# Masked self-attention with residual, one core: where the output products, the block turns, the mean and the fetches stand in the hand-written order

## The chip, the core and the metric

The kernel runs on 1 core of one Trainium2 chip. The metric is the device time of one execution in microseconds (us). Before the change it was measured at 685.06 us, the median of 3 runs (682.3 to 690.17). Five engines work side by side, each through a queue of its own in program order: PE (TensorE, matmuls; its weight loads are listed as PEld), DVE (VectorE), ACT (ScalarE), POOL (GpSimd) and SP (SyncE, which here only issues DMAs).

## What is computed

For each of 8 batches, `x` is 512 features by 1024 tokens, and a mask holds 0 or 1 for each token. With 8 heads of 64 features:

```python
xt = jnp.transpose(x, (0, 2, 1))
q = xt @ Wq.T
qh = q.reshape(B, T, NH, dk).transpose(0, 2, 1, 3)
scores = scale * jnp.einsum('bhqd,bhkd->bhqk', qh, qh)
logits = (scores * cmask + (1.0 - cmask) * NEG) * rmask
attn = jax.nn.softmax(logits, axis=-1)
ctx = jnp.einsum('bhqk,bhkd->bhqd', attn, qh)
out = ctx.transpose(0, 2, 1, 3).reshape(B, T, D) @ Wo.T
return x + jnp.transpose(out, (0, 2, 1))
```

`cmask` and `rmask` are the mask along keys and along queries. A masked key gets no weight; a masked query attends evenly to all tokens, so that its result is the mean over the tokens. Queries, keys and values are the same projection.

## The kernel before, in words

**Data.** Only the kept tokens of a batch are computed: up to 543 of them, gathered into NK = 544 columns, whose last column (number 543) holds the mean of all tokens. Every masked token of the batch takes its result from that column. `END` is 32, so a batch has five token blocks: four of 128 and one of 32 (`LAST`, number 4). Everything is float32.

**Turns.** The 8 heads of a batch make 4 pairs, so the work is 32 turns (b, pr), written out by hand under a manual schedule. A turn has five slots, k = 0 to 4. Slot k begins with the scores of one key block (slot 0 of the small block, slots 1 to 4 of blocks 0 to 3): matmuls of L669 and L691 into two PSUM tiles of tag "s" (two buffers, one for each head of the pair), then on ACT one exponential per head (L677), which frees the tile. After the scores, the slot's tasks are issued (`slots_of`, L1010 on), then the loads, searches, gathers and so on that tables in `late` name for (pr, k). Each engine takes its instructions in the order in which they were issued. So the order of calls is the order of the work, and whatever stands ahead of an exponential on ACT delays it.

**What a turn does beside its scores.** Slot 1 makes the values of the next pair. Slot 2 ends the weighted sums of the pair before (`end_attend`) and issues `lengths_of` for the next pair: ACT squares the values (L628), DVE adds them up and takes the maximum (L630, L637), for the bias of the exponentials. Slot 3 projects the first or second half of the queries of the pair after next (`project`, L583); with the second half of it, or with the first half in the turns pr = 2, goes the product of the maxima (`project_with_top`, `turn_top`, L640): PE turns DVE's maxima into the same PSUM bank, ACT copies the queries out (L593, L595), and DVE makes the bias (L649 to L652). After slot 4, `begin_attend` starts the weighted sums (L733) of the turn's own pair. The next turn starts with the scores of the small block (L691), which take the tile that the first head's exponential of slot 4 frees.

**Feature sums.** In slot 3 of the turns pr = 1 (for batch b + 1) and pr = 3 (for b + 2), behind the slot's tasks, ACT adds up four pieces of x (`add_features`, L492). DVE makes the mean's input from them after slot 4 of pr = 1 (`mean_of`, L497 and L499).

**The turns pr = 2.** Here the next batch's token blocks become columns: `collect` turns one block by four PE transposes (L551), and DVE or ACT copies it out (L555). Blocks 0 and 1 are in slot 2, blocks 2, 3 and 4 in slot 3 ahead of the projection with the maxima. Slot 1 has `put_mean`: four products of 128x32 by 128x4 (L566), one for each quarter of the partitions, and one DVE write (L569).

**Output.** `output` (L859) makes one token block of the previous batch: products of all four pairs' contexts with woT (L868), an ACT copy (L878), and DMAs to `od` in DRAM, issued by POOL (L880). Slot 3 of pr = 1 has blocks 0, 1 and LAST, pr = 2 has block 2, pr = 3 block 3, each behind the projection. All but block 0 are called with `wait=True`: their ACT copy is put off until after the scores of the next turn's slot 0. Two PSUM banks of tag "t" and two of tag "a" serve all of this.

**Way back.** Two batches later, POOL fetches the rows of `od` into eight blocks (`fetch`, L982, behind a one-element copy of an exponential, `keep_step`, L978, which ties it to the slot), and DVE turns each and adds x (`finish_blocks`, L942 and L945). The tables FETCH and FINISH give the slots.

**PSUM.** Eight banks: four for the scores, two "t", two "a".

Of the kernel before, what the change touches and what calls it, by code (L numbers as in the profile page):

```python
# [10 lines left out]
F32 = mybir.dt.float32  # L11
I32 = mybir.dt.int32
AF = mybir.ActivationFunctionType
ALU = mybir.AluOpType
AX = mybir.AxisListType
# [6 lines left out]
Q = 32  # L22
# [284 lines left out]
def attention_of_kept_tokens(ctx, tc, x, mask, wq, wo, out, ident, wqT, woT, verdict, flag):  # L307
# [37 lines left out]
    within = keep.tile([P, Q], F32, name="within")  # L345
# [214 lines left out]
    def put_mean(b, pm=None):  # L560

        xcs[b] = sb.tile([P, ND, NK], F32, tag="xc", name=f"xc_{b}", bufs=1)
        if pm is None:
            pm = bank(f"mean_{b}")
        for d in range(ND):
            nc.tensor.matmul(  # L566
                pm[d * Q : (d + 1) * Q, :A], within, xmeans[b][:, d, :], start=True, stop=True
            )
        nc.vector.tensor_scalar(xcs[b][:, :, NK - 1], pm[:, :A], 1.0 / T, None, ALU.mult)  # L569
# [287 lines left out]
    copies, rests = [], deque()  # L857

    def output(b, i, wait=False):  # L859
        n = sizes[i]  # L860
        if i == 0:
            ods[b] = dr.tile([NK, D], F32, tag="od", name=f"od_{b}")
        po = bank(f"po_{b}_{i}")
        parts = P // n
        w = D // parts
        for pr in range(ND):
            for k in range(parts):
                nc.tensor.matmul(  # L868
                    po[k * n : (k + 1) * n, :w],
                    cTs[b, pr][:, i * P : i * P + n],  # L870
                    woT[:, pr, k * w : (k + 1) * w],
                    start=(pr == 0),
                    stop=(pr == ND - 1),
                )

        def copy():
            oc = sb.tile([P, D], F32, tag="oc", name=f"oc_{b}_{i}", bufs=NC)
            nc.scalar.copy(oc[:, :w], po[:, :w])  # L878
            for k in range(parts):
                nc.gpsimd.dma_start(  # L880
                    ods[b][places[i], k * w : (k + 1) * w], oc[k * n : (k + 1) * n, :w]
                )

        if wait:
            copies.append(copy)
        else:
            copy()
# [122 lines left out]
    def slots_of(p):  # L1010
# [7 lines left out]
        def do(k, f, *args):  # L1018
            todo[k].append(lambda: f(*args))
# [19 lines left out]
        if before:  # L1039
            do(0, go_on_attend, before)  # L1040
        if p == 0:
# [18 lines left out]
        elif new:  # L1060
            do(1, mean_with_values)
            do(2, end_attend, before)
            do(2, collect, b + 1, 0, by_vector)
            do(2, collect, b + 1, 1)
            do(2, lengths_of, behind)
            do(3, collect, b + 1, 2, None, "a")
            do(3, collect, b + 1, 3, by_vector, "a")
            do(3, collect, b + 1, 4, by_vector)
            do(3, project_with_top, 0)
# [16 lines left out]
        if pr == 1 and b + 1 == B:  # L1086
            for i in range(LAST - 1):
                do((3, 3, 4)[i], output, b - 1, i)
        elif pr > 0 and 0 < b < B - 1:
            if pr == 1:  # L1090
                do(3, output, b - 1, 0)
            for i in {1: (1, LAST), 2: (2,), 3: (3,)}[pr]:
                do(3, output, b - 1, i, True)
# [30 lines left out]
    def early(n):  # L1124
# [37 lines left out]
        for ri in ris:  # L1162
# [8 lines left out]
            within, ident.rearrange("p (a f) -> p f a", a=A), axis=AX.X, op=ALU.add  # L1171
# [77 lines left out]
    def late(n):  # L1249
# [16 lines left out]
        for hf in range(2):  # L1266
# [15 lines left out]
            (0, 1): (0,),  # L1282
            (0, 2): (1,),
            (0, 3): (2,),
            (0, 4): (3,),
            (1, 0): (4, 5),
            (1, 1): (6, 7),
        }
        FINISH = {(0, 4): (0, 1), (1, 0): (2,), (1, 1): (3, 4), (1, 3): (5, 6), (1, 4): (7,)}
# [4 lines left out]
        for p, pair in enumerate(pairs):  # L1294
# [3 lines left out]
            for k, c in enumerate(order):  # L1298
                scores(pair, c)
                if k == 0:  # L1300
                    for copy in copies:
                        copy()
                    copies.clear()
# [196 lines left out]
```

## Time and profile before

| | |
|---|---|
| profiled execution, device time | 683.56 us |
| its span, first to last instruction | 681.8 us |
| median of the runs | 685.06 us (682.3 to 690.17) |
| mean granted TensorE clock | 0.973 |
| PE matmul busy | 627.0 us (92%) |
| DVE, ACT, POOL busy | 370.6, 386.7, 186.7 us |
| DMA | 116.55 MB, mean 171 GB/s |

How to read it: busy time is given for each engine, and a share of the span beside it. In lists of instructions, `x8` counts them, `[2.38 <-DVE top L637]` says that the engine sat idle for 2.38 us before this one and what released it. In lists of waits, the columns are the total in us, the number of times, and the longest. In rows for stretches of time, `PEclk` is the clock that TensorE was granted, as a share of full speed. Matmuls appear in two passes each, so a product of four matmuls is listed as x8.

### The profile page before, as it was taken

The page shows a single profiled execution, that of the slowest core. Times are in us where ns is not written, and L with a number is a line of the kernel's source. Part 1 is how long each engine was busy: PE and PEld are TensorE (multiplying, and loading weights), DVE is VectorE, ACT ScalarE, POOL GpSimd, SP SyncE. Part 2 cuts the span into 40 slices and gives each one's busy share as a digit, 9 for nine tenths or more (in the row PEclk, how much of TensorE's full clock was granted, in tenths as well). Part 3 has the DMA queues.
Part 4 walks back from the last instruction along what each step waited for, and adds up shares of the span by engine and source line. Part 5 has one row for each costly group of instructions (what it writes and reads, how often), then busy time and mean ns, then how long its engine had stood idle before and what let it go on. Part 6 is the DMA issues. An engine that isn't in the chain of part 4 may idle for free. (4 is left out here: it accounts for less than half of the span.)

```text
span 681.8 us, 15988 instructions
## 1 busy us (share of the span) xinstructions
PE 627.0 (92%) x6140; PEld 382.6 (56%) x6140; DVE 370.6 (54%) x1072; ACT 386.7 (57%) x1026; POOL 186.7 (27%) x313
## 2 busy tenths in 40 slices
PE   5798999999989999899998999799998999999974
PEld 4765665566654566556664566455664666645332
DVE  5446766246575455745576455745656423833742
ACT  3377767665764477574774477464774655536400
POOL 5620310310181103710172102810064102411421
PEclk9999999999997999999998999999998999999995
DMA  7553534443764687647875678648864653357656
GB/s 243 188 196 112 180 114 113 133 133 99 198 208 133 196 194 214 211 127 210 216 208 148 195 169 224 187 124 230 222 179 133 163 139 88 114 164 171 196 163 202
DMA packets 98671, 116.55 MB, mean 171 GB/s; under 512 B 10471, under 2 KB 76519, under 8 KB 98590
## 3 DMA queue, kind: packets, MB, share of 16 engines
q1 hardware_dynamic: 81742, 75.13, 41.5%
q0 software_dynamic: 12624, 38.25, 17.7%
q10 hardware_dynamic: 4224, 2.10, 1.0%
q8 instruction: 49, 0.80, 0.5%
q14 instruction: 32, 0.26, 0.1%
HBM read 72.78 MB, written 42.67 MB: 169 GB/s over the span
## 5 line engine op out<-in xcount | busy, mean ns | idle before, releaser
L677 ACT ACTIVATE e<-s,bias 128x544 f32<-128x544 f32 x256 | 180.5, 710 | 93.8 <-PE s L669 91.2
L669 PE MATMUL s<-qT 64*64 64x272 f32 x2048 | 151.9, 397 | 2.2 <-ACT e L677 0.8
L583 PE MATMUL pq<-xc,wqT 128*128 128x272 f32 x512 | 132.6, 403 | 4.4 <-ACT xc L555 4.4
L733 PE MATMUL av<-e,v 64*64 64x272 f32 x1920 | 130.9, 389 | 0.0
L583 PEld LDWEIGHTS pq<-xc,wqT 128*128 128x128 f32 x512 | 92.3, 190 | 40.0 <-issue 13.6
L880 POOL DMA_DIRECT2D od<-oc x56 | 29.9, 542 | 308.6 <-ACT oc L878 298.5
L868 PE MATMUL po<-woT,cT 128*128 128x512 f32 (+1 forms) x448 | 114.4, 453 | 0.0
L669 PEld LDWEIGHTS s<-qT 64*64 64x64 f32 x2048 | 74.9, 132 | 56.5 <-issue 16.0
L733 PEld LDWEIGHTS av<-e,v 64*64 64x64 f32 x1920 | 75.6, 133 | 37.8 <-issue 1.3
L868 PEld LDWEIGHTS po<-woT,cT 128*128 128x128 f32 (+1 forms) x448 | 50.2, 157 | 55.0 <-issue 48.3
L593 ACT COPY qT<-pq 128x272 f32<-128x272 f32 x64 | 24.7, 386 | 86.5 <-PE pq L640 45.1
L630 DVE TENSOR_REDUCE len<-sq 128x10 f32<-128x640 f32 x32 | 26.2, 818 | 81.1 <-ACT sq L628 81.1
L982 POOL DMA_INDIRECT g<-od,block_origin x56 | 57.3, 1024 | 29.8 <-DMA od<-oc 13.6
L677 ACT ACTIVATION_READ_ACCUMULATOR e<-s,bias 128x1 f32 x256 | 50.1, 196 | 0.0
L942 DVE STREAM_TRANSPOSE o<-g 128x512 f32<-128x512 f32 x56 | 39.3, 702 | 16.3 <-DMA g<-od,block_origin 16.0
L538 POOL DMA_INDIRECT xin<-xd,source x40 | 39.4, 984 | 14.3 <-DMA woT<-in_L_cond_Wq_dram 5.5
L945 DVE TENSOR_TENSOR xr<-o,xr 128x512 f32<-128x512 f32 x56 | 39.0, 696 | 1.9
L878 ACT COPY oc<-po 128x512 f32<-128x512 f32 (+1 forms) x35 | 17.5, 519 | 35.1 <-PE po L868 35.1
L473 DVE STREAM_TRANSPOSE xt<-x 128x1024 f32<-128x1024 f32 x28 | 34.8, 1242 | 4.0 <-DMA xd<-xt 3.6
L978 POOL COPY step<-e 1x1 f32<-1x1 f32 x75 | 16.5, 220 | 73.1 <-ACT e L677 72.6
L492 ACT ACTIVATE junka<-x 128x512 f32<-128x512 f32 x56 | 35.4, 631 | 1.3
L649 DVE TENSOR_REDUCE m<-pq 128x1 f32<-128x128 f32 x28 | 8.2, 292 | 50.3 <-ACT qT L595 33.7
(174 smaller groups left out, 702.8 us busy)
## 6 DMA issues: line engine op xcount, KB each, us to landing
xd<-xt SPq DMA_DIRECT2D x120, 128.0 KB
x<-in_x_dram SPq DMA_DIRECT2D x56, 256.0 KB
xr<-in_x_dram SPq DMA_DIRECT2D x28, 512.0 KB
out_dram<-xr SPq DMA_DIRECT2D x24, 512.0 KB
rb<-row SPq DMA_DIRECT2D x60, 160.0 KB
od<-oc POOLq DMA_DIRECT2D x28, 256.0 KB, 3.2
rank<-ranks SPq DMA_DIRECT2D x6, 512.0 KB
x<-in_x_dram POOLq DMA_DIRECT2D x8, 256.0 KB, 4.0
```

What stands on the lines that cost most here:

```text
L473: nc.vector.transpose(xt.rearrange("p k (d f) -> p k d f", d=ND), xs[b][r][:, :, at : at + n].rearrange("p d (k t) -> p k d t", t=Q),)
L492: nc.scalar.activation(junk, xs[b][r][:, d, :], AF.Copy, accum_out=xbars[b][:, d, r : r + 1])
L538: nc.gpsimd.indirect_dma_start(out=xin[:n, :], out_offset=None, in_=xds[b], in_offset=bass.IndirectOffsetOnAxis(ap=searches[b][2][:n, i : ...
L583: nc.tensor.matmul(pq[:, :KH], wqT[:, d, pr * P : (pr + 1) * P], xcs[b][:, d, cols], start=(d == 0), stop=(d == ND - 1),)
L669: nc.tensor.matmul(ss[h][r * DK : (r + 1) * DK, hf, :KH], qT[heads[h], c * P + r * DK : c * P + (r + 1) * DK], qT[heads[h], queries[hf]], ...
L677: nc.scalar.activation(e[:, :, h, :], ss[h][:, :, :KH], AF.Exp, bias=bias, scale=SCALE, accum_out=sums[pair[1] % 2][:, h, c : c + 1],)
L733: nc.tensor.matmul(avs[pair][hf][head, :KH], v[keys, c, head], e[keys, hf, h, :], start=(c == 0 and not crossed), stop=(c == LAST - 1 and ...
L868: nc.tensor.matmul(po[k * n : (k + 1) * n, :w], cTs[b, pr][:, i * P : i * P + n], woT[:, pr, k * w : (k + 1) * w], start=(pr == 0), stop=( ...
L880: nc.gpsimd.dma_start(ods[b][places[i], k * w : (k + 1) * w], oc[k * n : (k + 1) * n, :w])
L942: nc.vector.transpose(o.rearrange("p k t -> p (k t)"), gs[b, i])
L945: nc.vector.tensor_tensor(to, o, to, ALU.add)
L982: nc.gpsimd.indirect_dma_start(out=g, out_offset=None, in_=ods[b], in_offset=bass.IndirectOffsetOnAxis(ap=block_origin[:, b, i : i + 1], a ...
```

## The change

1. `output` no longer puts off its ACT copy. The list `copies`, and the loop that emptied it behind slot 0's scores, are gone.
2. In the turns pr = 1 and pr = 3 the output blocks stand at the head of slot 3's tasks, ahead of the projection with the maxima; in pr = 2 they stand behind the five collects and ahead of that projection. The last batch's pr = 1 has blocks 0 and 1 at the head of slot 3 too; its block 2 stays in slot 4.
3. In pr = 2, all five collects are in slot 3, blocks 0, 1, 2 and 4 copied by DVE, block 3 by ACT, and `lengths_of` comes behind them.
4. The mean: `within` is a 128x128 matrix (four copies of the 128x32 one), and one product of 128x128 by 128x16 takes the place of four; four DVE writes of 32 partitions each take the place of one.
5. FETCH and FINISH name other slots.

```diff
         if pm is None:
             pm = bank(f"mean_{b}")
+        nc.tensor.matmul(
+            pm[:, : ND * A],
+            within,
+            xmeans[b].rearrange("p d a -> p (d a)"),
+            start=True,
+            stop=True,
+        )
         for d in range(ND):
-            nc.tensor.matmul(
-                pm[d * Q : (d + 1) * Q, :A], within, xmeans[b][:, d, :], start=True, stop=True
-            )
-        nc.vector.tensor_scalar(xcs[b][:, :, NK - 1], pm[:, :A], 1.0 / T, None, ALU.mult)
+            rows = slice(d * Q, (d + 1) * Q)
+            nc.vector.tensor_scalar(
+                xcs[b][rows, :, NK - 1], pm[rows, d * A : (d + 1) * A], 1.0 / T, None, ALU.mult
+            )
...
-        def copy():
-            oc = sb.tile([P, D], F32, tag="oc", name=f"oc_{b}_{i}", bufs=NC)
-            nc.scalar.copy(oc[:, :w], po[:, :w])
...
-        if wait:
-            copies.append(copy)
-        else:
-            copy()
+        oc = sb.tile([P, D], F32, tag="oc", name=f"oc_{b}_{i}", bufs=NC)
+        nc.scalar.copy(oc[:, :w], po[:, :w])
+        for k in range(parts):
+            nc.gpsimd.dma_start(ods[b][places[i], k * w : (k + 1) * w], oc[k * n : (k + 1) * n, :w])
...
         if before:
             do(0, go_on_attend, before)
+        due = []
+        if pr == 1 and b + 1 == B:
+            due = [0, 1]
+        elif pr > 0 and 0 < b < B - 1:
+            due = {1: (0, 1, LAST), 2: (2,), 3: (3,)}[pr]
+        if not new:
+            for i in due:
+                do(3, output, b - 1, i)
...
             do(2, end_attend, before)
-            do(2, collect, b + 1, 0, by_vector)
-            do(2, collect, b + 1, 1)
-            do(2, lengths_of, behind)
-            do(3, collect, b + 1, 2, None, "a")
-            do(3, collect, b + 1, 3, by_vector, "a")
+            do(3, collect, b + 1, 0, by_vector)
+            do(3, collect, b + 1, 1, by_vector)
+            do(3, collect, b + 1, 2, by_vector, "a")
+            do(3, collect, b + 1, 3, None, "a")
             do(3, collect, b + 1, 4, by_vector)
+            do(3, lengths_of, behind)
+            for i in due:
+                do(3, output, b - 1, i)
             do(3, project_with_top, 0)
             do(3, project, ahead, 1, None, "a")
...
         if pr == 1 and b + 1 == B:
-            for i in range(LAST - 1):
-                do((3, 3, 4)[i], output, b - 1, i)
-        elif pr > 0 and 0 < b < B - 1:
-            if pr == 1:
-                do(3, output, b - 1, 0)
-            for i in {1: (1, LAST), 2: (2,), 3: (3,)}[pr]:
-                do(3, output, b - 1, i, True)
+            do(4, output, b - 1, 2)
...
         FETCH = {
-            (0, 1): (0,),
-            (0, 2): (1,),
-            (0, 3): (2,),
-            (0, 4): (3,),
-            (1, 0): (4, 5),
+            (0, 0): (0,),
+            (0, 1): (1,),
+            (0, 2): (2,),
+            (0, 3): (3,),
+            (0, 4): (4,),
+            (1, 0): (5,),
             (1, 1): (6, 7),
         }
-        FINISH = {(0, 4): (0, 1), (1, 0): (2,), (1, 1): (3, 4), (1, 3): (5, 6), (1, 4): (7,)}
+        FINISH = {(0, 4): (0, 1), (1, 1): (2, 3), (1, 2): (4, 5), (1, 4): (6, 7)}
...
             for k, c in enumerate(order):
                 scores(pair, c)
-                if k == 0:
-                    for copy in copies:
-                        copy()
-                    copies.clear()
```

More of the change, by code (lines that the diff above doesn't have):

```diff
@@ L344, in attention_of_kept_tokens @@
     quadrant = keep.tile([P, A], F32, name="quadrant")
-    within = keep.tile([P, Q], F32, name="within")
+    within = keep.tile([P, P], F32, name="within")
     key = keep.tile([P, NC], F32, name="key")
@@ L856, in attention_of_kept_tokens, with output @@
     ods, gs, xrs = {}, {}, {}
-    copies, rests = [], deque()
-    def output(b, i, wait=False):
+    rests = deque()
+    def output(b, i):
         n = sizes[i]
@@ L874, in output @@
                 )
-        def copy():
-            oc = sb.tile([P, D], F32, tag="oc", name=f"oc_{b}_{i}", bufs=NC)
[L878 to L881, printed above, removed]
-                )
-        if wait:
-            copies.append(copy)
-        else:
-            copy()
+        oc = sb.tile([P, D], F32, tag="oc", name=f"oc_{b}_{i}", bufs=NC)
+        nc.scalar.copy(oc[:, :w], po[:, :w])
+        for k in range(parts):
+            nc.gpsimd.dma_start(ods[b][places[i], k * w : (k + 1) * w], oc[k * n : (k + 1) * n, :w])
     partials = {}
@@ L1170, in early @@
         nc.vector.tensor_reduce(
-            within, ident.rearrange("p (a f) -> p f a", a=A), axis=AX.X, op=ALU.add
+            within[:, :Q], ident.rearrange("p (a f) -> p f a", a=A), axis=AX.X, op=ALU.add
+        )
+        nc.vector.tensor_copy(
+            within[:, Q:].rearrange("p (a f) -> p a f", f=Q),
+            within[:, :Q].unsqueeze(1).to_broadcast([P, A - 1, Q]),
         )
```

## The prediction

> **What bounds the kernel now.** I read the page's busy times first, then the waits of PE, then the turns around the longest of them in order of time, and the granted clock in short stretches.
>
> ```profile
> span 681.8 us, 15988 instructions
> PE 627.0 (92%) x6140; PEld 382.6 (56%) x6140; DVE 370.6 (54%) x1072; ACT 386.7 (57%) x1026; POOL 186.7 (27%) x313
> ```
>
> PE is the bound: only what lets PE run without a pause, or at a higher clock, moves the end. So the list of waits is read for PE's rows; the others show what comes late.
>
> ```profile
> POOL od L880 <- ACT oc L878: 298.5, 28, 18.8
> PEld pq L640 <- DVE top L637: 18.6, 6, 4.7
> DVE o L942 <- DMA g<-od,block_origin: 16.0, 7, 3.8
> PE pq L640 <- DVE top L637: 16.0, 6, 4.3
> PE s L691 <- ACT e L677: 4.5, 3, 1.8
> PE pq L583 <- ACT xc L555: 4.4, 6, 0.7
> ```
>
> The largest, 16.0 us, is the product of the maxima. It comes once in each turn pr = 1 from b = 2 on (five long waits; the sixth, in the last batch, is 0.19). In order of time, b = 3:
>
> ```profile
> 278.69 0.73 ACT L628 ACTIVATE sq<-v 128x640 f32<-128x640 f32 x1
> 282.01 0.70 DVE L942 STREAM_TRANSPOSE o<-g 128x512 f32<-128x512 f32 x1
> 283.36 0.81 DVE L630 TENSOR_REDUCE len<-sq 128x10 f32<-128x640 f32 x1
> 284.43 0.32 PE L640 MATMUL pq<-ident,top 128*128 128x128 f32 x1 [2.38 <-DVE top L637]
> 284.59 8.04 PE L868 MATMUL po<-woT,cT 128*128 128x512 f32 x48
> ```
>
> The squares are there at 279.42, but DVE finishes two fetched blocks first, so the maxima are late; then come 8.04 us of output products that need no maxima. That order is the fault which the change turns around.
>
> The wait costs more than its length. Stretches of 3.41 us, set so that they end where the matmuls change pace (columns: PE busy, clock):
>
> ```profile
> 50.96:54.37 3.41, 1.90 (x33) 1.00 0.58 154
> 201.14:204.56 3.42, 1.28 (x6) 1.00 0.65 193
> 204.56:207.97 3.41, 1.99 (x4) 0.50 0.80 228
> 283.06:286.48 3.42, 2.05 (x6) 1.00 0.75 210
> 286.48:289.89 3.41, 3.41 (x9) 1.00 0.84 275
> 358.16:361.57 3.41, 0.83 (x3) 1.00 0.86 219
> 361.57:364.98 3.41, 3.41 (x5) 0.50 0.93 270
> ```
>
> Where PE was busy for 1.28 us or less of such a stretch, the next ran at clock 0.50; after 1.90 and 2.05 it stayed at 1.00. So the limit lies between 1.28 and 1.90. The same 48 passes that took 8.04 us above then took:
>
> ```profile
> 206.25 10.59 PE L868 MATMUL po<-woT,cT 128*128 128x512 f32 x48
> 360.90 9.74 PE L868 MATMUL po<-woT,cT 128*128 128x512 f32 x48
> ```
>
> One slow stretch costs 9.74 - 8.04 = 1.70 us (half of 3.41); two in a row cost 2.55 here, as PE was still waiting in part of the first. Of the five long waits, four were followed by slow stretches: 2.55 + 3 x 1.70 = 7.7 us.
>
> **The change, part by part.**
>
> *Output products ahead of the maxima, pr = 1.* PE has 8.04 us of products before it needs the maxima, against a longest wait of 4.3. All 16.0 us go, and with them the 7.7 us of slow clock. The weight loader waited 18.6 us in the same place, so restarting costs up to 2.6 more; I take 1. Sum -24.7.
>
> *What is late next.* In slot 3 the feature sums stand on ACT behind the projection's copies, and the copies behind the maxima; the exponentials of slot 4 stand behind the sums. Before, PE did output products while ACT added features. Now nothing lies between the projection and slot 4's scores. The trace has this very order already: batch 0, pr = 1, which has no output products.
>
> ```profile
> 64.40 0.27 PE L640 MATMUL pq<-ident,top 128*128 128x128 f32 x1
> 64.71 0.39 ACT L593 COPY qT<-pq 128x271 f32<-128x271 f32 x1 [0.64 <-PE pq L640]
> 65.12 0.64 ACT L492 ACTIVATE junka<-x 128x512 f32<-128x512 f32 x1
> 65.68 0.27 PE L1245 MATMUL home_t<-ident,home 64*128 64x64 f32 x1
> 67.40 0.63 ACT L492 ACTIVATE junka<-x 128x512 f32<-128x512 f32 x1
> 68.03 0.69 ACT L677 ACTIVATE e<-s,bias 128x544 f32<-128x544 f32 x1
> 68.86 0.69 PE L691 MATMUL s<-qT 64*64 64x272 f32 x8 [1.83 <-ACT e L677]
> ```
>
> From the maxima's product to the next turn's first scores: 68.86 - 64.40 = 4.46 us, set by ACT (copies, four sums from 65.12 to 68.03, an exponential). Without feature sums (b = 3, pr = 0) it is 270.63 - 268.39 = 2.24:
>
> ```profile
> 268.39 0.27 PE L640 MATMUL pq<-ident,top 128*128 128x128 f32 x1
> 270.63 0.69 PE L691 MATMUL s<-qT 64*64 64x272 f32 x8
> ```
>
> So each turn with feature sums and no products behind the maxima loses 2.22 us. Before the change pr = 3 hides it:
>
> ```profile
> 327.24 0.27 PE L640 MATMUL pq<-ident,top 128*128 128x128 f32 x1
> 327.35 3.60 PE L868 MATMUL po<-woT,cT 128*128 128x512 f32 x8
> 332.06 0.71 ACT L677 ACTIVATE e<-s,bias 128x544 f32<-128x544 f32 x1 [1.10 <-PE s L669]
> 332.92 0.69 PE L691 MATMUL s<-qT 64*64 64x272 f32 x8
> ```
>
> There ACT waits 1.10 us for PE; pr = 1 hides it with block 1 and the small block. Both covers go: in pr = 1 of b = 1 to 6 and, for nothing in return, in pr = 3 of b = 1 to 5 (later batches have no features to add). 11 x 2.22 = +24.4. Lower bound: three waits of this kind in batch 0 sum to 4.5, so 11 x 1.5 = 16.5; upper bound: 11 x 4.46 = 49, if PE had nothing to do meanwhile. I take 2.22, since the chain is the same instruction by instruction.
>
> *The clock after the new waits.* A new wait leaves PE idle for 1.83 + 0.20 (a product that only batch 0 has, from 65.68 to 65.88) = 2.03 us. If it falls into one stretch, 3.41 - 2.03 = 1.38 us of work are left, near the 1.28 that was slowed. The stretches run on a clock of their own, so it falls wholly inside with a chance of (3.41 - 2.03) / 3.41 = 0.40; with the limit half way, at 1.59, a little may spill over and it is 0.53. Of 11, six: +10.2 us. Bounds: none, 0, and all, 18.7. [...]
>
> *Collects in one slot, pr = 2.*
>
> ```profile
> L569 DVE TENSOR_SCALAR xc<-mean 128x4 f32<-128x4 f32 x8 | 1.3, 164 | 6.4 <-PE mean L566 6.4
> ```
>
> ```profile
> 298.26 0.24 PE L566 MATMUL mean<-mean,within 128*32 128x4 f32 x8
> 302.88 0.69 DVE L555 COPY xc<-xc 128x512 f32<-128x512 f32 x1 [4.14 <-PE xc L551]
> 306.48 2.10 PE L583 MATMUL pq<-xc,wqT 128*128 128x272 f32 x8 [0.74 <-ACT xc L555]
> 310.36 3.60 PE L868 MATMUL po<-woT,cT 128*128 128x512 f32 x8
> ```
>
> The transposes are the same in number. The 0.74 us before the projection are covered by block 2's 3.60 us: -4.4 over six turns. The maxima come behind four DVE copies now (three of 0.69, one short: about 2.4 us from the first turned block), then about 1 us of L630 and L637: 3.4. Until PE asks for them it has the other transposes, 3.60 of products and 2.10 of projection. No wait by that, with over 2 us to spare; without the products in between it would be 1.3 in each of six turns.
>
> *DVE's queue.* FINISH puts two blocks, not one, behind the feature sums of pr = 1 (283.36 - 282.01 = 1.35 us more). The sums end up to 2.2 us later, as the turn is longer by their wait, and there are three more mean writes (0.5 us). That is 4.1 us more ahead of the collects' copies. DVE idled 4.14 us there, and the first collect now comes later by a slot's scores. So nothing is taken; up to 1 us a turn if the cover is short.
>
> *Mean.* Eight passes in 0.24 us become two: between 0 and -1.7 over seven turns; I take -0.7, as one loading of weights stays.
>
> *Copies, od writes, fetches.* The ACT copies leave slot 0, where PE lost nothing to them. POOL waits 298.5 us in all for such copies and gets them earlier; each od write still takes one issue, and behind it stand only later fetches. Fetches come a slot earlier, the first right behind slot 0's scores; od's last block is copied more than a slot before. If the first fetch did wait for it, it would hold up POOL, not PE: its block is finished four slots later. DVE's 16.0 us of waits for fetched blocks shrink, on an engine with room. SP's queue is not changed. The wider `within` is one DVE copy while the mask is loading: 0.
>
> Sum against the profiled execution's 683.56: -24.7 + 24.4 + 10.2 - 4.4 - 0.7 = +4.8, so 688.4, say 688. The median of the runs is 685.06, 1.5 above that execution; by it the forecast is +0.4%. It is taken against the execution, since it replaces waits of that execution, and the new waits do not depend on what a fetch takes.
>
> **Rivals.** *No slow clock.* All as above, but the new waits stay below the limit: 683.56 - 24.7 + 24.4 - 5.1 = 678.2, faster by 1%. For it: 1.38 lies above 1.28, and a wait may be split over two stretches, as that of 2.38 at 282.05 was (2.05 busy). Against: the margin over 1.28 is 0.10. It decides if the limit lies below 1.38. [...]
>
> *Every new wait is slowed* (slower): as it costs half a stretch each time, the turns may keep step with the stretches. 11 x 1.70 = 18.7 in place of 10.2: 697. For it: the same turns follow at the same distances. Against: the wait of 2.38 went free. It decides from nine of eleven.
>
> *The feature sums do not reach PE.* If ACT had room, 24.4 + 10.2 would go: 654. Against: the batch 0 rows show the wait.
>
> *The maxima stay late.* The wait moves to pr = 2 behind the collects: up to 1 to 2 us in six turns, 694 to 700. Against: the cover counted above.
>
> **How the numbers follow.** About 1% is what a measurement of this kernel can tell from no change: 6.9 us, so below 678.2 and above 691.9. Forecast, four to eight slow stretches, 685 to 692: 0.55. No slow clock, 678: 0.20, half of it on either side of the line. All slowed, 693 to 698: 0.10. Maxima or DVE late: 0.08. No wait on ACT, 654: 0.07. Faster 0.10 + 0.07, and 0.03 for a run with few slow stretches: 0.20; slower 0.10 + 0.08 and 0.05 from the upper edge of the forecast: 0.23; the rest, 0.57, within 1%. The range holds the forecast and no slow clock, and the lower part of the slower cases: 677 to 695.
>
> **What would show it.** Right: no wait at the product of the maxima; eleven new waits of about 2.0 us at the small block's scores, released by the exponential, ACT in feature sums ahead of it; five to seven stretches of clock 0.50, now behind those; the 0.74 gone. Wrong: the sums ending before slot 4's scores, a clock of 1.00 throughout, or PE waiting for xc or for the maxima in pr = 2.

## The result, and the profile after

The changed kernel takes 710.76 us (median of 4 runs, 708.35 to 712.45), the kernel before 686.61 (4 runs, 682.3 to 690.17): a ratio of 1.035, 95% interval 1.028 to 1.042. The forecast was 688 and no change; the time lies above its range of 677 to 695. The profiled execution has a span of 709.4 us.

The page's first lines:

```profile
span 709.4 us, 15944 instructions
PE 635.6 (90%) x6092; PEld 388.4 (55%) x6092; DVE 377.9 (53%) x1103; ACT 385.5 (54%) x1020; POOL 187.7 (26%) x313
```

PE issues 48 passes fewer and is busy for 8.6 us more. Part of this is clock: 0.969 of 709.4 us against 0.973 of 681.8, some 3.6 us. Part is waiting that is counted as busy: in the turns pr = 1 of batches 2 to 6 PE is busy for 22.3 to 22.4 us, and for 21.59 where the exponentials start on time (finished blocks first, below). The span grew by 27.6 us. PE's own waits:

```profile
PE s L698 <- ACT e L684: 28.8, 14, 2.2
PE s L676 <- ACT e L684: 7.5, 6, 1.7
PE pa L895 <- DVE cT L859: 7.4, 1, 7.4
```

The wait for the maxima (16.0 us) and the six of 0.74 us are gone from this list. In their place stand eleven of 2.2 us at the small block's scores (the other three of the 14 are batch 0's), six at the scores of slots 1 to 4 (four of 1.3 to 1.7 us in pr = 2 of batches 2, 3, 5 and 6, the other two in batch 0), and one of 7.4 us in the last turn. In the list of all engines' waits, three rows tell what else moved:

```profile
DVE m L656 <- ACT qT L602: 99.8, 21, 10.3
ACT v L624 <- DVE xc L574: 13.2, 6, 3.2
DVE total L497 <- ACT junka L492: 12.8, 6, 2.1
```

DVE now stands for up to 10.3 us at the bias (before: up to 2.3), since the maxima's product comes behind 8 us of output products. And ACT waits for DVE's write of the mean before it copies values, which it did not do before.

Where the time went is seen from the turns. The table adds their lengths over batches 1 to 6 (a turn runs from its first small-block matmul, line 698 or 691, to the next turn's), with the four turns of batch 0 and those of batch 7, to the end, in one column each; the 39 us ahead of the first turn are left out. Some kernels of the experiments stand in it.

| us | batch 0 | pr = 0 | pr = 1 | pr = 2 | pr = 3 | batch 7 |
|---|---|---|---|---|---|---|
| before | 65.1 | 81.4 | 153.1 | 127.9 | 101.6 | 113.8 |
| before, profiled again | 65.9 | 81.4 | 147.2 | 127.9 | 101.6 | 116.7 |
| changed | 67.3 | 88.0 | 146.9 | 132.7 | 112.7 | 122.7 |
| features first | 63.9 | 81.2 | 129.7 | 135.5 | 101.6 | 114.7 |
| finish first | 65.1 | 88.0 | 142.7 | 122.9 | 112.7 | 113.4 |
| pr = 3 as before | 65.2 | 81.4 | 142.7 | 134.2 | 101.6 | 114.4 |
| changed, profiled a fourth time | 67.2 | 86.6 | 148.1 | 134.4 | 112.7 | 119.9 |
| the same, plain fetches | 66.5 | 86.4 | 142.7 | 136.0 | 112.7 | 114.7 |
| both first | 68.0 | 82.1 | 133.7 | 121.2 | 101.6 | 114.0 |
| both first, fetches spread | 68.1 | 83.2 | 130.9 | 121.2 | 101.6 | 114.4 |

From before to changed: +2.2, +6.7, -6.3, +4.8, +11.1, +8.9, in sum 27.4 of the 27.6.

**The slow clock.** Stretches of 3.41 us (columns: PE busy, clock), the first two around the wait behind pr = 3 of batch 1, the last two around that of batch 3:

```profile
180.98:184.39 3.41, 1.20 (x24) 1.00 0.96 316
184.39:187.80 3.41, 3.41 (x36) 0.52 0.20 50
344.82:348.23 3.41, 1.73 (x32) 1.00 1.05 356
348.23:351.64 3.41, 3.41 (x35) 1.00 0.73 193
```

Five of the eleven new waits were punished, each with 1.20 to 1.24 us of work in its stretch and 0.52 or 0.53 as the clock of the next; 1.73 went free. Four of the five slow stretches lie in pr = 0, which is 13.49 us long without and 15.14 to 15.18 with: +1.66 each, the 6.7 of the table. The fifth lies in pr = 2 of batch 4, where PE would have stood for 1.5 us in any case, so that turn is no longer than its neighbours (22.44).

### The profile page after: what moved, and what is told of

It is laid out like the page before. It is cut to its first block, busy times and chain, and to the rows that moved or that the text cites. A ratio compares the mean times of both kernels' runs of the same rounds, so it can differ in the third digit from the quotient of the medians.

```text
span 709.4 us, 15944 instructions
## 1 busy us (share of the span) xinstructions
PE 635.6 (90%) x6092; PEld 388.4 (55%) x6092; DVE 377.9 (53%) x1103; ACT 385.5 (54%) x1020; POOL 187.7 (26%) x313
## 3 DMA queue, kind: packets, MB, share of 16 engines
q0 software_dynamic: 12624, 38.25, 16.8%
## 4 chain that ended last, share of the span: by engine, by line
PE 76%; DVE 7%; ACT 7%; issue 4%; DMA 3%; another core or an unknown queue 1%; SPq 1%; POOL 0%; POOLq 0%; ACTq 0%; DVEq 0%
PE pq L590 18%; PE s L676 17%; PE po L875 15%; PE av L740 11%; ACT e L684 4%; PE av L722 3%; PE s L698 3%; PE xc L551 2%; PE pa L895 2%; PE v L618 2%; ACT junka L492 2%; DMA x<-in_x_dram 1%; PE warm L431 1%; DVE xt L473 1%
## 5 line engine op out<-in xcount | busy, mean ns | idle before, releaser
L676 PE MATMUL s<-qT 64*64 64x272 f32 x2048 | 163.7, 408 | 9.7 <-ACT e L684 7.5
L740 PE MATMUL av<-e,v 64*64 64x272 f32 x1920 | 136.5, 398 | 0.2 <-remote 0.2
L676 PEld LDWEIGHTS s<-qT 64*64 64x64 f32 x2048 | 78.3, 136 | 67.0 <-ACT e L684 22.4
L875 PE MATMUL po<-woT,cT 128*128 128x512 f32 (+1 forms) x448 | 108.9, 439 | 0.0
L740 PEld LDWEIGHTS av<-e,v 64*64 64x64 f32 x1920 | 77.6, 135 | 40.3 <-issue 4.0
L875 PEld LDWEIGHTS po<-woT,cT 128*128 128x128 f32 (+1 forms) x448 | 46.5, 149 | 54.6 <-issue 53.4
L981 POOL DMA_INDIRECT g<-od,block_origin x56 | 55.3, 988 | 19.9 <-issue 10.0
L698 PE MATMUL s<-qT 64*64 64x272 f32 x256 | 22.8, 413 | 29.0 <-ACT e L684 28.8
L977 POOL COPY step<-e 1x1 f32<-1x1 f32 x75 | 18.6, 248 | 91.5 <-ACT e L684 90.2
```

The costliest lines, as they stand in the source:

```text
L676: nc.tensor.matmul(ss[h][r * DK : (r + 1) * DK, hf, :KH], qT[heads[h], c * P + r * DK : c * P + (r + 1) * DK], qT[heads[h], queries[hf]], ...
L698: nc.tensor.matmul(s[to, h, :KH], qT[heads[h], keys], qT[heads[h], queries[hf]], start=True, stop=True)
L740: nc.tensor.matmul(avs[pair][hf][head, :KH], v[keys, c, head], e[keys, hf, h, :], start=(c == 0 and not crossed), stop=(c == LAST - 1 and ...
L875: nc.tensor.matmul(po[k * n : (k + 1) * n, :w], cTs[b, pr][:, i * P : i * P + n], woT[:, pr, k * w : (k + 1) * w], start=(pr == 0), stop=( ...
L981: nc.gpsimd.indirect_dma_start(out=g, out_offset=None, in_=ods[b], in_offset=bass.IndirectOffsetOnAxis(ap=block_origin[:, b, i : i + 1], a ...
```

## Experiments

"Changed" is the kernel after the change; each edit is made to it unless said otherwise.

**Feature sums first.** In slot 3 of pr = 1 and pr = 3, ahead of the output blocks:

```diff
+        if pr == 1 and b + 1 < B:
+            for i in range(G):
+                do(3, add_features, b + 1, G + i)
+        if pr == 3 and b + 2 < B:
+            for i in range(G):
+                do(3, add_features, b + 2, i)
         if not new:
```

> The changed kernel, with the feature sums of pr = 1 and pr = 3 issued at the head of slot 3, ahead of the output products, instead of behind the slot's tasks. Theory (feature sums behind the projection's copies hold up slot 4's exponentials): the eleven waits of 2.2 us at the small block's scores go (24.3 us), with them the slow stretches behind them (five of 1.66, 8.3 us) and about 2 us in batch 0; turns pr = 3 of 16.9 us and pr = 1 of about 22.4; time about 676 against 710.8. The 2 us lost in each turn pr = 2 stay, because the mean is late for another reason. Rival (the copies of the queries themselves hold up the exponentials, whatever stands behind them): the waits stay, 710.

667.62 us, 0.975 of before (0.968 to 0.981). All fourteen waits at the small block but two short ones are gone:

```profile
PE s L676 <- ACT e L684: 7.2, 6, 1.6
PE s L698 <- ACT e L684: 2.6, 2, 1.5
```

Turns pr = 3 are 16.93 each, pr = 1 21.63, and no slow stretch lies in pr = 0. The first theory holds: it is the sums behind the projection's copies. Pr = 2 kept its loss, as expected.

**Finished blocks first.**

```diff
-        FINISH = {(0, 4): (0, 1), (1, 1): (2, 3), (1, 2): (4, 5), (1, 4): (6, 7)}
+        FINISH = {(0, 4): (0, 1), (1, 1): (2, 3), (1, 2): (4, 5, 6, 7)}
```

> The changed kernel, with the finished blocks 6 and 7 moved from slot 4 of pr = 1 (behind the bias on DVE, which waits for the output products) to slot 2 of pr = 1 (ahead of it). Theory (DVE reaches the mean's write in pr = 2 late because 2.7 us of finished blocks stand behind the bias, and ACT's value copy waits for that write): turns pr = 2 of b = 2 to 6 go from 22.4-22.8 to 20.2-20.5 us, the 1.3-us waits at the scores go, 10 us in all; the rows of batch 5 are finished before the output products, so that the stores, the load of x and the last spread copy come earlier and the wait of 7.4 us in the last turn shrinks by 3 or more; about 697. Rival (pr = 2 is longer because of the five collects in one slot): turns pr = 2 stay at 22.4, 707 to 711.

685.92 us, 1.003 (0.999 to 1.006). Pr = 2 fell to 20.2 us a turn, below the 21.3 of before. How it comes is seen in DVE's rows. Changed, batch 3 (the turn pr = 2 begins at 304.90):

```profile
304.19 0.16 DVE L497 TENSOR_TENSOR total<-xbar 128x4 f32<-128x4 f32 x1 [2.14 <-ACT junka L492]
304.48 0.70 DVE L941 STREAM_TRANSPOSE o<-g 128x512 f32<-128x512 f32 x1
...
306.56 0.69 DVE L944 TENSOR_TENSOR xr<-o,xr 128x512 f32<-128x512 f32 x1
...
311.53 0.68 DVE L574 TENSOR_SCALAR xc<-mean 32x4 f32<-32x4 f32 x4
```

ACT and PE of the changed kernel at the same place:

```profile
312.30 0.27 ACT L624 COPY v<-mean 128x128 f32<-128x128 f32 x1 [2.82 <-DVE xc L574]
```

```profile
313.81 1.83 PE L676 MATMUL s<-qT 64*64 64x272 f32 x16 [1.31 <-ACT e L684]
```

And the kernel before (its turn begins at 294.66):

```profile
291.72 0.16 DVE L497 TENSOR_TENSOR total<-xbar 128x4 f32<-128x4 f32 x1 [2.94 <-ACT junka L492]
...
298.58 0.17 DVE L569 TENSOR_SCALAR xc<-mean 128x4 f32<-128x4 f32 x1 [0.77 <-PE mean L566]
```

Before, DVE was ready for the mean 0.77 us early and wrote it 3.92 us into the turn. Now it comes 6.63 us in: feature sums 2.2 us later, one finished block more. ACT's value copy reads the same PSUM tile and waits for the write; the exponentials behind it are late, and PE stands. With the blocks moved, the write is 3.93 us into the turn again:

```profile
303.02 0.68 DVE L574 TENSOR_SCALAR xc<-mean 32x4 f32<-32x4 f32 x4
```

**Pr = 3 as before.** Its output block back behind the projection, its copy put off:

```diff
+            if pr == 3:
+                for i in due:
+                    do(3, output, b - 1, i, True)
```

> The changed kernel, with the output block of pr = 3 back behind the projection and its ACT copy put off to the next turn, as before the change. Theory: turns pr = 3 of b = 1 to 5 go from 19.16 to 16.93 us (11.1 us) and the slow stretches behind four of them go (6.7 us): 693. Rival (pr = 3 is longer for another reason of the change, as the tables): no change, 710.

679.51 us, 0.995 (0.991 to 1.000). Pr = 3 fell by 11.1 and pr = 0 by 6.7, as expected, but the kernel by 31.

**Tables as before** (FETCH and FINISH of the kernel before):

> The changed kernel with the tables FETCH and FINISH of before the change. Theory: three finished blocks, not two, then stand behind the bias in pr = 1, so the mean comes 1.35 us later: turns pr = 2 of about 23.8, six times, and the last turn's wait is longer by 1 to 3: about 720. If the late exponentials in slots 1 and 2 of pr = 1 (0.8 us each turn from b = 2 on) come from the new fetch table, 5 us come back there: 715. Rival (the tables are what makes pr = 2 long): turns pr = 2 fall to 20.3-21.3: 700 or less.

692.32 us, 1.013 (1.005 to 1.020). That is below the rival's 700, but what the next paragraph tells of has part in it. Pr = 2 did not get longer, it fell to 21.55 from batch 3 on. Two of the three blocks stand in slot 3, where DVE waits 2.14 us for the feature sums in any case (the row of L497 above), so only one is left behind them. My expectation had missed that.

**A third cause.** All four of these variants took less than was expected, the first three by 8, 11 and 13 us. The turns show where: pr = 1 of 23.79 against 24.6 (21.63 with the feature sums first), batch 0's pr = 2 of 18.1 against 20.2 (with the tables of before 19.8, a slow stretch in it), the last turn 57 to 58 against 65.3. So the changed kernel was measured again, with other variants beside it.

> The changed kernel once more, nothing edited. In its first profile, exponentials in slots 1 and 2 of pr = 1 (b from 2 on) began 0.8 us after their scores with nothing left to wait for, batch 0 lost 2 us in pr = 2, and the last turn took 65.3 us; none of this is in the four variants measured since, each of which changes one other thing. If the kernel itself does this, the same rows are there again and the time is 708 to 713. If it belongs to that chip or that loading of the program, turns pr = 1 are 23.8, batch 0's pr = 2 is 18.1, the last turn 57 to 58, and the time is about 14 us less: 694 to 699.

711.17 us, 1.035 (1.025 to 1.045), with the same late exponentials. The other three of this series have them too:

> Both edits together: feature sums at the head of slot 3, finished blocks 6 and 7 in slot 2 of pr = 1. Theory: the two losses are independent, so pr = 1 stays at 21.63 and pr = 3 at 16.93, and the turns pr = 2 of b = 2 to 6 go from 22.4-24.0 to about 20.2, with the two slow stretches there: 15 us less than the feature sums alone (667.6), and 1 in the last turn: about 652. Rival (with the feature sums early, DVE is still late for the mean): pr = 2 stays above 21.5, 661 to 668.

665.53 us, 0.967 (0.959 to 0.975), 13.5 above the theory: pr = 2 fell as expected, pr = 1 grew to 22.4 to 23.5, and batch 0's pr = 2 takes 24.2.

> The kernel before, with one thing of the change: in pr = 1 of b = 1 to 6 the three output blocks stand ahead of the projection, their copies made at once. By the theory the wait for the maxima goes and turns pr = 1 are 23.8 (142.7 for six, against 153.1), with a wait of 2.2 us at the end of each; one or two slow stretches behind them cost 2 to 3; finished blocks 5, 6 and 7 stand behind the bias on DVE, so turns pr = 2 lengthen by 0.2 to 2 us each: 676 to 687. The prediction's own steps for this part alone (24.7 off, 6 x 2.2 on, three slow stretches on) give 684 - 24.7 + 13.2 + 5 = 677. Rival (the wait for the maxima only moves to another place): 686 or more.

This is the kernel before with

```diff
+        if pr == 1 and 0 < b < B - 1:
+            for i in (0, 1, LAST):
+                do(3, output, b - 1, i)
```

and no products behind the projection in pr = 1. 705.97 us, 1.023 (1.006 to 1.040), 19 above the upper end. The wait for the maxima is gone, but pr = 1 adds up to 164.5: its exponentials in slots 1 and 2 start up to 2.7 us late, while POOL issues up to five indirect fetches in a row.

> The changed kernel with the mean as before: four products and one write on DVE in place of one product and four writes. Theory: the write is done 0.5 us earlier, so ACT's value copy and the turns pr = 2 of b = 2 to 6 gain 0.5 each, less 0.2 for the products: 1 to 3 us less than the changed kernel in this call. Rival (the mean's form does not matter): within 1 us of it.

706.54 us, 1.026 (1.016 to 1.037): 4.6 less than the changed kernel beside it, where 1 to 3 were expected. Pr = 2 fell by 3.2 in its profile, 0.6 a turn from batch 3 on: the four writes cost about what they take (0.68 against 0.17). Other stages of the two profiles differ by as much (pr = 0 by 3.4 less, batch 7 by 1.8 more), so the other 1.4 are not accounted for.

Then the changed kernel and the edits side by side:

> The changed kernel beside three variants on one chip. The late exponentials (0.8 us in slots 1 and 2 of pr = 1) were there in all four profiles of the last series and in none of the series before. If they belong to the kernel, they are here in this one and not in the finished-blocks-first variant: 708 to 713 against 685. If they go with the chip, both have them or neither has: the difference between the two is then 10 to 14 us, as theory said, either about 697 and 685 or about 710 and 697.

> Finished blocks 6 and 7 in slot 2 of pr = 1, as before, beside the changed kernel on the same chip. Theory: 10 to 14 us less than the changed kernel of this series (six turns pr = 2 of 20.2 against 22.4, and 1 to 4 in the last turn). Rival (the variant as such has no late exponentials): 25 less, as the two first profiles had it.

> Both edits, as before, beside the changed kernel on the same chip. Theory: the losses of feature sums (24.3 and 8.3 of slow clock, 2 in batch 0) and finished blocks (10 to 14) add up: 45 to 49 less than the changed kernel of this series; about 652 where the exponentials are on time, about 665 where they are late.

708.23, 692.77 and 664.38 us (1.034, 1.011, 0.971 of before). Finishing first is worth 15.5 where the exponentials are late, both edits 43.9, nearly the 45 expected. In the two profiles, finishing first takes 8.1 off pr = 2 (134.3 to 126.2) and 7.7 off the last turn (63.96 to 56.27). The same kernel with finished blocks first took 685.92 in the first series and 692.77 here: its exponentials are late in one and not in the other. Lateness went by the series, that is by which kernels were run together: none in the four profiles of the first, some in every profile of the later ones. It is not tied to one chip: chip 5 ran the first four without and, later, four others with it.

> Both edits, and all eight fetches in pr = 0 (one or two in each slot), none in pr = 1. If POOL's indirect DMAs issued beside a slot's exponentials are what makes those late, turns pr = 1 are 21.63 in all of b = 1 to 6, on any chip; where both edits alone have late exponentials, this one gains about 5 us on them in pr = 1 and may lose some of it in pr = 0, where two fetches stand in a slot. Rival (the fetches have nothing to do with it): no difference from both edits alone beyond 2 us.

677.85 us, 0.987 (0.982 to 0.991), 13 more than without this edit (its profiled execution took 683.61). One turn of it, PE's scores, the last of five indirect fetches in a row, and ACT:

```profile
423.11 1.48 PE L676 MATMUL s<-qT 64*64 64x272 f32 x16
...
426.84 0.98 POOL L981 DMA_INDIRECT g<-od,block_origin  x1 [0.16 <-issue]
...
428.52 0.71 ACT L684 ACTIVATE e<-s,bias 128x544 f32<-128x544 f32 x1 [5.22 <-PE pq L618]
```

The scores end at 424.6, the fetches at 427.8, and the exponential starts at 428.5. Behind this row of five the exponential is 3.9 us late, behind the rows of two of the changed kernel 0.7 to 0.9; moving them together was the wrong way.

**Plain fetches, and untied ones.** First the changed kernel, as the measure:

> The changed kernel again, as the measure for the three beside it on this chip: 708 to 713 and exponentials 0.7 to 0.8 us late in slots 1 and 2 of pr = 1, or, on a chip like that of the first series, 696 and none late.

710.11 us, and late exponentials. In the next, a plain DMA stands in place of each indirect fetch:

```diff
-        nc.gpsimd.indirect_dma_start(
-            out=g,
-            out_offset=None,
-            in_=ods[b],
-            in_offset=bass.IndirectOffsetOnAxis(ap=block_origin[:, b, i : i + 1], axis=0),
-        )
+        nc.gpsimd.dma_start(g, ods[b][i * 32 : i * 32 + P, :])
```

> The changed kernel with each indirect fetch replaced by a plain DMA of 128 rows that lie together, issued by POOL in the same place (it leaves out the reordering of rows). If POOL's work on indirect DMAs, 0.97 us each, is what holds up the exponentials beside it, none is late in pr = 1 from b = 2 on, and those turns are 23.79: 4 to 5 us less than the changed kernel. If the traffic of the fetch or the copy that ties it to the slot does it, they stay late.

700.72 us, 9.4 less. Changed (first profile), batch 4, slot 1 of pr = 1, PE, then POOL, then ACT:

```profile
361.88 1.10 PE L676 MATMUL s<-qT 64*64 64x272 f32 x16
```

```profile
360.90 0.97 POOL L981 DMA_INDIRECT g<-od,block_origin  x1 [0.16 <-issue]
...
362.26 0.97 POOL L981 DMA_INDIRECT g<-od,block_origin  x1 [0.17 <-issue]
```

```profile
361.36 0.20 ACT L703 ACTIVATE share<-bias 128x4 f32<-128x4 f32 x1
363.75 0.72 ACT L684 ACTIVATE e<-s,bias 128x544 f32<-128x544 f32 x1 [2.19 <-PE s L676]
```

The scores end at 362.98, ACT is free from 361.56, the exponential waits for nothing else, and starts at 363.75. With plain fetches, the same place:

```profile
361.02 1.10 PE L676 MATMUL s<-qT 64*64 64x272 f32 x16
```

```profile
362.15 0.71 ACT L684 ACTIVATE e<-s,bias 128x544 f32<-128x544 f32 x1 [1.45 <-PE s L676]
```

It starts 0.03 us after the scores' end, and so it is in every turn pr = 1 from batch 1 to 6 (23.79 each). That this execution was simply one without lateness is ruled out by its batch 0, whose gathers are still indirect: two exponentials beside them are 0.4 us late, and pr = 2 takes 19.3 us there, against 18.1 in the first series. The last turn fell from 62.5 to 58.0. In the first profile of the changed kernel that turn shows what happens: eight fetches in a row, and ACT's copy of the inverses behind them.

```profile
643.26 1.02 POOL L981 DMA_INDIRECT g<-od,block_origin  x1 [2.28 <-DMA od<-oc]
...
652.51 0.96 POOL L981 DMA_INDIRECT g<-od,block_origin  x1 [0.16 <-issue]
```

```profile
647.08 1.31 PE L802 MATMUL rb<-ident,ris 128*64 128x128 f32 x20
...
654.77 0.75 ACT L809 COPY rb<-rb 128x512 f32<-128x512 f32 x2 [6.33 <-remote]
```

It stands for 6.33 us with its input ready at 647.08 + 1.31 = 648.4, DVE's contexts come behind it, and PE's 7.4 us at L895 behind those. Before the change, the first of these eight was issued 23.9 us after the start of pr = 2, and ACT's copy made at 23.3; now they are issued from 18.4 on, ahead of it. In the second run of finished blocks first, whose exponentials are late too, they start at 22.9, only 0.4 ahead of the copy, which is made at 23.3 without a wait, and the last turn takes 56.3: what is lost there depends on where the eight fall.

Without the copy that ties a fetch to its slot:

```diff
                     for i in FETCH.get((pr, k), ()):
-                        keep_step(pair, c)
                         fetch(b - 2, i)
```

> The changed kernel without the one-element copy on POOL that ties each fetch to its slot, so that POOL reads no exponentials ahead of a fetch and fetches as soon as od is written. If that copy is what holds up the next exponentials, none is late in pr = 1: 4 to 5 us less. If the fetches themselves do it, they are late elsewhere, where the fetches now fall, and the time is within 3 us of the changed kernel or longer.

752.68 us, 42.6 more. The fetches bunch up, six in a row here, and eight in batch 7, where an exponential starts 8.9 us after its scores:

```profile
366.89 1.02 POOL L981 DMA_INDIRECT g<-od,block_origin  x1 [0.27 <-POOL part L400]
...
373.24 0.95 POOL L981 DMA_INDIRECT g<-od,block_origin  x1 [0.30 <-issue]
```

```profile
375.52 0.71 ACT L684 ACTIVATE e<-s,bias 128x544 f32<-128x544 f32 x1 [4.33 <-remote]
```

```profile
376.38 2.32 PE L676 MATMUL s<-qT 64*64 64x272 f32 x14 [4.94 <-ACT e L684]
```

PE itself stands too in this kernel, in the middle of a row of matmuls and with nothing that the profile shows to wait for, while six fetches run (192.00 to 199.30):

```profile
196.38 0.93 PE L590 MATMUL pq<-xc,wqT 128*128 128x272 f32 x3 [0.77 <-issue]
197.82 0.94 PE L590 MATMUL pq<-xc,wqT 128*128 128x272 f32 x3 [0.51 <-issue]
```

So it is neither the volume of the traffic, which is the same with plain fetches (38.25 MB on POOL's queue in both), nor the tying copy, but POOL's indirect DMAs, and how many follow each other (0.7 to 0.9 us late behind two in the changed kernel, 4.3 behind six here). (Plain fetches also read rows that lie together; that their pattern rather than their form matters was not tested apart.)

**Versions that gain.** Both edits with the old fetch table (two fetches in slot 0 of pr = 1), and with one fetch in each slot:

> Feature sums and finished blocks first, with the fetch table of before the change (each fetch of pr = 0 one slot later, blocks 4 and 5 in slot 0 of pr = 1). Theory (the fetch table matters little): 661 to 666, as both edits alone. Rival (fetches in pr = 1 make its exponentials late): slot 0 of pr = 1 has two of them, so turns pr = 1 are longer by up to 1 us each: 668 to 672.

676.75 us, 0.989 (0.980 to 0.999), above both. The first exponential of slot 1, behind the two fetches of slot 0 and the one before them, is 2.2 us late in three turns. With one fetch in each slot:

```diff
             (1, 0): (5,),
-            (1, 1): (6, 7),
+            (1, 1): (6,),
+            (1, 2): (7,),
```

> Feature sums and finished blocks first, with the fetch of block 7 one slot later (slot 2 of pr = 1), so that no slot has two fetches. If two indirect DMAs behind each other are what makes the exponentials of slot 1 to 2 late, those of slot 2 are on time: turns pr = 1 of b = 2 to 6 about 0.7 shorter where they were late, 661 against 664 to 666. If one is enough, or the gathers of slot 2 now stand behind it: no gain, 664 to 668.

658.77 us, 0.967 (0.962 to 0.973). That is the shortest time, but on another chip: as a share of the kernel before beside it, it is no better than both edits alone (0.967 and 0.971). What the profile shows is 2.8 us less in pr = 1 (130.9 against 133.7), of which pr = 0 takes back 1.1. Slot 2's exponentials are on time, slot 1's are late by 0.7 still, and slot 3's are now late by 1.1 to 1.8, behind the fetch of slot 2 and the gathers that follow it at once. Batch 2, PE, POOL and ACT:

```profile
202.95 8.15 PE L875 MATMUL po<-woT,cT 128*128 128x512 f32 x48
203.21 0.97 POOL L538 DMA_INDIRECT xin<-xd,source  x1 [0.16 <-issue]
204.24 0.71 ACT L684 ACTIVATE e<-s,bias 128x544 f32<-128x544 f32 x1 [1.24 <-PE s L676]
```

Still, of the turns pr = 1 of batches 2 to 6 four are as short as without any lateness (21.63 to 21.65), for PE has 8.15 us of output products to do meanwhile. Where a late start falls decides its price. In slot 1 alone it costs next to nothing: in the fourth profile of the changed kernel, batch 5 has it there only and takes 23.85, against 23.79 on time, while batch 4 has it in slot 2 too and takes 24.57. The largest loss of this kind that is left in the kernels that gain is in batch 0, whose pr = 2 takes 22.2 to 24.2 behind its gathers, against 18.1.

**The kernel before, profiled again.**

> The kernel before, profiled once more, nothing edited. In its first profile no exponential of the turns was late, though it has as many indirect fetches as the changed kernel. If its own order keeps the fetches away from the exponentials, none is late here either, and the time is 682 to 690. If the first profile only fell on a good loading of the program (as the four variants of the first series seem to have done), some are late by 0.7 us or more, and its time is at the upper end, 688 to 692.

682.58 us (one run), but another way of getting there:

```profile
PE s L669 <- ACT e L677: 3.9, 6, 1.5
PE pq L640 <- DVE len L630: 1.2, 1, 1.2
```

The wait for the maxima, 16.0 us in the profile of the prediction, is 1.2 here. Instead exponentials are late by up to 3.3 us in pr = 1:

```profile
194.91 1.71 PE L669 MATMUL s<-qT 64*64 64x272 f32 x16
...
199.22 0.71 ACT L677 ACTIVATE e<-s,bias 128x544 f32<-128x544 f32 x1 [3.69 <-PE pq L611]
```

It starts 2.6 us after its scores' end (194.91 + 1.71). The maxima themselves come no earlier: they are ready 13.4 to 15.9 us into the turns pr = 1 of batches 2 to 6, and were 13.7 to 15.7 in the first profile. But PE gets to them 1.8 to 4.2 us later than there, held up by ACT, and so hardly waits for them. In both profiles POOL issues five fetches in a row as pr = 1 begins; they cost time in either kind of execution, once through DVE and the maxima, once through ACT.

## Why the prediction was wrong

**Right.** The wait for the maxima and its slow clock go, and the new waits come: pr = 1 should change by -24.7 + 6 x 2.22 = -11.4, and where no exponential is late it is -10.4 (142.7). Eleven waits were forecast, eleven came, 2.20 to 2.21 us each; pr = 3 grew by 11.1, which is 5 x 2.22. The features-first kernel shows that the reason was the right one. Of the slow stretches six were forecast, five came, and they cost 6.7 us in place of 10.2. That the number came so near is in part luck: the forecast rested on a limit put half way between two stretches, and one of the five fell where it cost nothing. Stretches with 1.20 us of work were enough to lose the clock here, as those with 0.83 and 1.28 were in the trace of before. That the stretches keep a time of their own, on which the chance in the forecast rested, is seen in both profiles: the slow ones within the turns begin 157.0, 78.5 and 78.5 us apart before (46, 23 and 23 times 3.413), and 81.9, 119.5, 41.0 and 81.9 us apart after (24, 35, 12 and 24 times).

**Wrong: the step "DVE's queue", "nothing is taken".** Its size was right, "4.1 us more" (feature sums 2.2 later, one block of 1.35, the writes 0.5), its cover was not. It held them against the 4.14 us that DVE idled ahead of the collects' copies. But another instruction stands ahead of those in the same queue, the write of the mean, where DVE idled 0.77 us, and ACT waits for it. 4.1 - 0.77 = 3.3; the write and ACT's copy of the values came some 3 us later, and pr = 2 cost +4.8 in place of -5.1. That is 9.9 us, and moving two finished blocks ahead of the bias takes 9.8 off pr = 2 (122.9), or 8.1 where it ran beside the changed kernel (134.3 to 126.2).

**Wrong: the step "Copies, od writes, fetches", "it would hold up POOL, not PE".** The step asked only who waits for the data, and put the move of the fetches at nothing. The trace of before had no row in which an indirect DMA of POOL held ACT up. In the changed kernel it costs some 4 us in pr = 1 (146.9 against 142.7; the other 1 of the 5.1, from -11.4 to -6.3, is missing even where none is late), most of the 8.9 in the last batch, and the 2.2 of batch 0, where it is the gathers, which the change left where they were: about 15 us at most. Plain fetches took back 10.7 us of span. They did not touch batch 0's gathers, and there exponentials stay late.

**Also wrong: the -24.7 as such.** It is what one execution lost. In the other kind PE loses the time ahead of the maxima, to late exponentials, and the reordering, which does not touch those, has less to win: 147.2 before, 146.9 after. Between these two profiles, both with late exponentials, the stages differ by +1.4, +6.6, -0.3, +4.8, +11.1 and +6.0. A second profile would have shown that the wait of 16.0 us is not always there.

Added up: the 4.8 of the forecast, +9.9 for DVE, +5.1, +8.9 and +2.2 for ACT behind the fetches and gathers, -3.5 for the slow clock: 27.4, against 27.6. The sum closes because each term is the difference of a stage; what shows the causes are the edits that took the terms back. Why some executions have late exponentials and others none stays open, and with it why the first profile of before had none.

## What to carry to other kernels

When work is pushed later in an engine's queue, look for the first instruction behind it that some other engine waits for, and take the idle time in front of that one as the cover: here the 0.77 us ahead of the mean's write counted, and the 4.14 us further on covered nothing. When independent work is put ahead of a wait, go through what then has none in front of it, on ACT and DVE too: here feature sums had to move along, and the two edits together turned 3.5% slower into 3% faster. Keep indirect DMAs apart, gathers and fetches alike, and put them where the engine that paces the kernel has work of its own ahead of the next result from ACT: here an exponential began 0.7 to 0.9 us late behind two in a row and 3.9 behind five, one fetch a slot in place of two took pr = 1 from 133.7 us to 130.9, and with 8.15 us of output products to do meanwhile four of five turns were as short as without lateness. And profile twice before a wait is taken for a term of the sum: the one of 16.0 us was 1.2 in the second profile.

## What the runs showed of the hardware

Behind POOL's indirect DMAs (0.97 us each on POOL), ACT starts instructions late for which the profile shows nothing left to wait for: by 0.7 to 0.9 us behind two in a row (changed kernel, pr = 1), by 2.2 behind three (both edits with the old fetch table), by up to 3.9 behind five (all fetches in pr = 0), by 4.3 behind six (untied fetches), and by 6.3 and 8.9 where eight follow each other (last batch of the changed kernel and of the untied fetches). With plain DMAs issued by POOL in the same places (0.55 us each on POOL) the exponential starts 0.03 us after its scores, and the turns pr = 1 of batches 1 to 6 take 23.79 us each. In the kernel with the untied fetches PE stands too, for 0.5 to 0.8 us at a time. ACT's late starts were there in fourteen profiles, and in the one with plain fetches beside the gathers that stayed indirect; in five others (the first of the kernel before, and the four of the first series) no exponential is late, though these kernels have as many fetches. What differs between these executions, and by which way POOL's work reaches ACT, stays open: for the executions that have it, the runs showed that plain fetches took it out of pr = 1 and that longer rows came with later starts.
